# Earlier due time for the last graph, a shorter DVE hop and a shorter hold in the planner, and one activation less at the front

## The chip, the cores and the metric

The kernel runs on one core of a Trainium2 chip. A core has a matrix engine (TensorE, in the profile PE, its weight loads PEld), a vector engine (DVE), a scalar engine (ACT), a general engine (POOL) and a queue processor that only issues transfers (SP). Each engine takes its instructions in the order in which the program has them. The metric is the device time of one execution in microseconds (us), as a median of several runs.

## The reference

64 graphs of 256 nodes with 256 features each go through four layers, each behind a layer norm and a relu and each added to the residual `x`:

```
x = x + gat0(relu(ln(x)), adj)      # 4 heads, softmax over neighbours, elu
x = x + gat1(relu(ln(x)), adj)      # 4 heads, typed edges, relu, residual, layer norm per head
x = x + gat2(relu(ln(x)), adj)      # 1 head of 256
x = x + ggnn(relu(ln(x)), adj)      # 3 rounds: m = h W_i; aggr = A^T m; h = GRU(aggr, h)
```

`adj` holds only 0 and 1. No graph needs another graph, but inside a graph everything is one long chain, and the last layer is the costliest: three rounds of a GRU with six 256 x 256 products each, of which every round needs the state that the round before left.

## The kernel before

**Units.** The 64 graphs are cut into 33 units: one lone graph at the front (unit 0), 31 pairs (units 1 to 31), one lone graph at the end (unit 32). `graphs(u, first, nb)` writes down all operations of a unit: `layer0`, `layer1`, `layer2` and `gru`. A pair's operations work on 512 columns, a lone graph's on 256.

**The steps on TensorE**, with the lines by which the profile knows them. A *projection* (L1219, up to four row blocks) multiplies the turned, normed rows `ht` with the layer's weights. A *row* step (L1276) turns one column of scores into a row; it is a single short matmul. *Attend* (L1365) multiplies softmax weights `pt` with the projected rows; for the four-headed layers it uses half of the array's columns (`128*64` in the profile), two heads in one planner operation. In the GRU a *gate* product (L1587) is one planner operation of two matmuls of 512 columns, each of which the profile shows as two records; twelve gate operations make a round. *Aggregate* (L1566) is the product with the adjacency. A transpose through TensorE stands at L1180 (normed rows) and L1624 (the state of a lone graph).

**Turning a pair's rows.** For pairs in the middle, rows are not turned on TensorE: ACT copies them apart into two 16-bit planes (`pl<-xn`, `pl<-ht`, L1168), SP issues a transposing transfer (`tp<-pl`, L1197 and L1604), and ACT (for `ht`) or DVE (for `y`) joins the planes again. For the last unit (`ENDED = 1`) and for the first ones the rows go through TensorE (L1180) and one ACT copy. Between two rounds of a pair's GRU the state goes `ht`, `pl`, `tp`, `y`, `hl`, aggregate; between two rounds of the lone graph it goes L1624, `hl`, aggregate.

**The order is planned.** The kernel holds its own planner, `_Schedule`. Every operation has a cost, and a due time worked back from the end of its unit, `sched.end[u]`, through the operations that need it. The planner then plays the program through on a model of the engines: whenever an engine is idle, it takes, among the operations whose inputs are ready and whose buffers are free, the one with the earliest due time. The order in which it does this is the order in which the program issues on every engine, SP's and ACT's transfers too. The unit ends are 100000 ns apart for a pair (`PACE`), later than the kernel needs, so that they only rank the units. Two of the planner's numbers matter here. `HOP` is the time that it lets pass from the end of an operation until another engine may use the result. `HOLD` is about the array's two shapes: a change between full-width matmuls and the half-width attend costs time, so on TensorE the planner keeps to the present shape as long as there is work of that shape due no more than `HOLD` ns after the most urgent one (unless two attends of the half-width shape are waiting, `TOGETHER`).

**The front.** The DMA issues on ACT for the weight vectors, a one-column `Exp` activation named `warm` (L880), then the first norm. Every DMA issue uses one of eight completion counters in turn and waits until the transfer that used the counter before has landed.

Of the kernel before, what the change touches and what calls it, by code (L numbers as in the profile page):

```python
# [9 lines left out]
F32 = mybir.dt.float32  # L10
# [3 lines left out]
AF = mybir.ActivationFunctionType  # L14
# [521 lines left out]
LEAVE = 0  # L536
PACE = 100000.0
FIRST = 0.0
SINGLES = 1, 1
LAG = 6000  # L540

# [24 lines left out]
class _Schedule:  # L566
# [9 lines left out]


    OVERLAP = {"pe": 0, "act": 97, "dve": 81, "pool": 0, "sp": 0}
    HOP = {"pe": 300, "act": 100, "dve": 100, "pool": 100, "sp": 0}
    DMA_LATENCY = 3500  # L580
    DMA_RATE = 220.0
    DMA_AHEAD = 2000
# [4 lines left out]
    GUARDED = ("wh","cb2_")  # L587
    STRICT = ("hl",)
    STICK = 0.0
    HOLD = 10000.0  # L590
    TOGETHER = 2
    SWITCH = {True: 0.0, False: 0.0}

# [118 lines left out]
    def run(self):  # L712
# [18 lines left out]
        def post(t, kind, o):  # L731
            nonlocal count
            count += 1
            heapq.heappush(events, (t, count, kind, o))
# [6 lines left out]
        while True:  # L741
            for e in engines:
# [9 lines left out]
                if e == "pe" and not halves:  # L752
                    stick = self.HOLD if sum(ops[i].halves for _, i in able[e]) < self.TOGETHER else 0.0
                while able[e]:
# [40 lines left out]
            while events and events[0][0] == clock:  # L795
                _, _, kind, o = heapq.heappop(events)
                if kind == "free":
# [5 lines left out]
                    else:  # L803
                        post(clock + self.OVERLAP[o.engine] + self.HOP[o.engine], "done", o)
                    if o.engine == "pe":
# [13 lines left out]
def _fast_path(  # L819
# [34 lines left out]
    nc = tc.nc  # L854
# [3 lines left out]
    P = 128  # L858
# [3 lines left out]
    units = [  # L862
        *((g, 1) for g in range(SINGLES[0])),
        *((g, 2) for g in range(SINGLES[0], B - SINGLES[1], 2)),
        *((g, 1) for g in range(B - SINGLES[1], B)),
    ]
# [4 lines left out]
    consts = ctx.enter_context(tc.tile_pool(name="consts", bufs=1))  # L871
# [3 lines left out]
    ones = consts.tile([P, P], F32, name="ones")  # L875
    nc.gpsimd.memset(ones, 1.0)
    ident = consts.tile([P, P], F32, name="ident")
    make_identity(nc, ident)
    warm = consts.tile([P, 1], F32, name="warm")
    nc.scalar.activation(warm, ones[:, :1], AF.Exp)  # L880
    nhalf = consts.tile([P, C * H], F32, name="nhalf")
    nc.gpsimd.memset(nhalf, -0.5)
    viol = consts.tile([P, B + 1], F32, name="viol")
# [16 lines left out]
    sched = _Schedule(  # L900
        tc,
        {
            "xt": (slots, 6), "at": (slots, 1), "am": (slots, 6), "cap": (slots, 4),
            "cap_n": (slots, 1), "xn": (slots, 3), "ht": (slots, 2), "wh": (slots, 3),
            "cb2_": (slots, 2), "cb1_": (slots, 1), "pt": (slots, 4), "o": (slots, 2),
            "ag": (slots, 2), "ht3_": (slots, 3), 
            "hl": (slots, 2), "am_r": (slots, 1), "g": (slots, 7), "y": (slots, 2), "f": (slots, 6),
            "st": (slots, 4), "mv": (slots, 6), "row": (slots, 3), "col": (slots, 4), "rs": (slots, 10),
# [791 lines left out]

    for u, (first, nb) in enumerate(units):
        sched.group = u
        sched.end[u] = (first + nb) * PACE / 2 - (FIRST if u == 0 else 0.0)
        graphs(u, first, nb)


# [23 lines left out]
@with_exitstack  # L1730
def kernel(ctx: ExitStack, tc: tile.TileContext, *args):
    nc = tc.nc
    keep = ctx.enter_context(tc.tile_pool(name="keep", bufs=1))
    flag = keep.tile([1, 1], I32, name="flag")
    _fast_path(tc, *args, flag)
    taken = nc.values_load(flag[0:1, 0:1])
    with tc.If(taken > 0):
        _general_path(tc, *args)
# [38 lines left out]
```

## Time and profile before

| what | value |
|---|---|
| median of 3 runs | 2981.08 us (2980.25 to 2981.66) |
| the profiled execution | 2981.97 us, of which the span of its instructions 2980.2 us |
| TensorE busy | 2944.9 us, 99% |
| ACT, DVE busy | 2361.1 us (79%), 2357.4 us (79%) |
| TensorE busy in 0 to 60 us, 60 to 120 us | 45.13 of 60, 54.49 of 60 |
| TensorE busy in 300 to 2540 us | 2237.84 of 2240 |
| TensorE busy in 2700 us to the end | 267.87 of 281 |
| last TensorE instruction ends | 2973.65 us |

Section 1 of the page has the busy times, section 2 the span in 40 slices, section 4 the chain of work that ended last. In the timeline every line is one instruction or a run of like ones: when it starts, how long it lasts, the engine, the line of the kernel, the operation, `written<-read`, the shape, and in brackets how long the engine was idle just before, and what ended that.

### The profile page before, as it was taken

The page shows a single profiled execution, that of the slowest core. Times are in us where ns is not written, and L with a number is a line of the kernel's source. Part 1 is how long each engine was busy: PE and PEld are TensorE (multiplying, and loading weights), DVE is VectorE, ACT ScalarE, POOL GpSimd, SP SyncE. Part 2 cuts the span into 40 slices and gives each one's busy share as a digit, 9 for nine tenths or more (in the row PEclk, how much of TensorE's full clock was granted, in tenths as well). Part 3 has the DMA queues.
Part 4 walks back from the last instruction along what each step waited for, and adds up shares of the span by engine and source line. Part 5 has one row for each costly group of instructions (what it writes and reads, how often), then busy time and mean ns, then how long its engine had stood idle before and what let it go on. Part 6 is the DMA issues. An engine that isn't in the chain of part 4 may idle for free.

```text
span 2980.2 us, 47482 instructions
## 1 busy us (share of the span) xinstructions
PE 2944.9 (99%) x16927; PEld 1754.7 (59%) x16927; DVE 2357.4 (79%) x5605; ACT 2361.1 (79%) x4404; POOL 304.0 (10%) x315
## 2 busy tenths in 40 slices
PE   8999999999999999999999999999999999999998
PEld 6765556555555555555555565555565555555555
DVE  7968877788877789777788877888777887777764
ACT  7976887888888788787888878888887987876654
POOL 2101010111110111101010101111001010000000
PEclk9999999999999999999999999999999999999999
DMA  4322533434434333433434334344343333332211
GB/s 125 85 60 67 110 86 72 107 72 100 92 76 110 78 83 89 98 85 78 94 80 100 86 75 109 69 96 93 79 106 78 82 89 93 76 74 59 51 43 28
DMA packets 560537, 248.37 MB, mean 83 GB/s; under 512 B 487130, under 2 KB 540196, under 8 KB 560292
## 3 DMA queue, kind: packets, MB, share of 16 engines
q1 hardware_dynamic: 556320, 243.88, 35.7%
q8 instruction: 137, 2.24, 0.3%
q10 hardware_dynamic: 3972, 1.36, 0.2%
q14 instruction: 108, 0.88, 0.1%
HBM read 109.84 MB, written 17.34 MB: 43 GB/s over the span
## 4 chain that ended last, share of the span: by engine, by line
PE 96%; ACT 2%; DVE 1%; DMA 0%; issue 0%; SPq 0%; ACTq 0%
PE bank L1587 65%; PE bank L1365 12%; PE bank L1219 11%; PE bank L1566 6%; ACT ht L1168 1%; ACT g L921 1%; PE bank L1045 0%; PE bank L1254 0%; PE bank L1276 0%; PE bank L1180 0%; DMA w0e<-in_L_gnn_W_dram 0%; DVE g L921 0%; DVE o L921 0%; DVE pt L921 0%; ACT xn L1124 0%
## 5 line engine op out<-in xcount | busy, mean ns | idle before, releaser
L1587 PE MATMUL bank<-ht,whh 128*128 128x512 f32 (+1 forms) x2376 | 1048.8, 581 | 1.3 <-DVE ht L921 1.0
L1587 PE MATMUL bank<-ag,wc 128*128 128x512 f32 (+1 forms) x2376 | 1037.6, 581 | 0.0
L1587 PEld LDWEIGHTS bank<-ag,wc 128*128 128x128 f32 x2376 | 445.1, 190 | 502.3 <-issue 474.5
L1587 PEld LDWEIGHTS bank<-ht,whh 128*128 128x128 f32 x2376 | 436.1, 190 | 438.0 <-issue 408.4
L921 ACT ACTIVATE g<-bank,bg 128x512 f32<-128x512 f32 (+1 forms) x594 | 395.6, 672 | 262.4 <-PE bank L1587 253.4
L921 DVE SCALAR_TENSOR_TENSOR g<-g,g 128x512 f32<-128x512 f32 (+1 forms) x396 | 263.6, 672 | 290.4 <-ACT g L921 289.4
L1365 PEld LDWEIGHTS bank<-wh,pt 128*64 128x64 f32 (+1 forms) x8704 | 344.2, 141 | 82.3 <-issue 61.6
L1365 PE MATMUL bank<-wh,pt 128*64 128x65 f32 (+1 forms) x8704 | 375.3, 232 | 1.5 <-DVE pt L921 1.5
L921 DVE SCALAR_TENSOR_TENSOR pt<-pt,f,cap 128x256 f32<-128x256 f32 x640 | 280.9, 480 | 108.5 <-ACT pt L1339 107.9
L1339 ACT ACTIVATE pt<-cb,f 128x256 f32<-128x256 f32 x640 | 334.7, 597 | 1.7 <-PE bank L1365 1.4
L1168 ACT COPY ht<-tp 128x1024 uint16<-128x1024 uint16 x232 | 301.8, 1335 | 0.0
L921 POOL TENSOR_TENSOR mv<-mv,nhalf 128x4 f32<-128x4 f32 (+1 forms) x132 | 144.4, 1094 | 1179.5 <-DVE mv L1110 916.0
L1566 PE MATMUL bank<-am_r,hl 128*128 128x256 f32 x1536 | 246.4, 309 | 0.0
L1168 ACT COPY pl<-xn 128x1024 uint16<-128x1024 uint16 x232 | 234.9, 1043 | 0.0
L1566 PEld LDWEIGHTS bank<-am_r,hl 128*128 128x128 f32 x1536 | 198.5, 188 | 48.2 <-issue 38.7
L921 POOL TENSOR_TENSOR mean<-mean,nhalf 128x8 f32<-128x8 f32 (+1 forms) x66 | 142.2, 2161 | 793.0 <-DVE mean L921 754.8
L1124 ACT ACTIVATE xn<-xt,mv 128x256 f32<-128x256 f32 x384 | 173.4, 500 | 56.0 <-DVE mv L921 48.5
L921 ACT ACTIVATE g<-g,bg 128x512 f32<-128x512 f32 (+1 forms) x198 | 136.8, 705 | 79.2 <-DVE g L921 78.8
L1168 ACT COPY pl<-ht 128x1024 uint16<-128x1024 uint16 x186 | 191.5, 1040 | 6.1 <-DVE ht L921 5.3
L1229 ACT ACTIVATE wh<-bank,mv 128x264 f32<-128x264 f32 (+1 forms) x384 | 172.0, 482 | 29.0 <-PE bank L1219 27.0
L921 DVE BATCH_NORM_STATS2 st<-xt 128x6 f32<-128x256 f32 x512 | 185.7, 413 | 6.4 <-DMA xt<-in_x_dram 6.2
L1330 DVE TENSOR_SCALAR pt<-cb,f 128x256 f32<-128x256 f32 x512 | 184.0, 408 | 8.3 <-ACT cb L1262 4.6
(104 smaller groups left out, 3163.9 us busy)
## 6 DMA issues: line engine op xcount, KB each, us to landing
cb<-rd SPq DMA_DIRECT2D x120, 512.0 KB, 4.7
xt<-in_x_dram SPq DMA_DIRECT2D x31, 512.0 KB, 5.0
at<-in_adj_dram SPq DMA_DIRECT2D x31, 512.0 KB, 4.9
out_dram<-xt SPq DMA_DIRECT2D x31, 512.0 KB, 2.9
cb<-rd SPq DMA_DIRECT2D x34, 256.0 KB, 3.2
tp<-pl SPq DMA_TRANSPOSE x418, 3.1
cap<-cap_n SPq DMA_TRANSPOSE x128, 3.0
rd<-row ACTq DMA_DIRECT2D x60, 8.0 KB, 2.3
```

Of the source, the lines that this page charges most:

```text
L921: emit = lambda: fn(*[a() if callable(a) else a for a in args], **kw)
L1124: op("act", 505, lambda: nc.scalar.activation(view(), xt.tile[:, c, :], AF.Relu, bias=mv.tile[:, 3, c : c + 1], scale=2.0 if MERGED else 1 ...
L1168: op("act", cost, lambda: nc.scalar.copy(to(), of()), reads, writes)
L1219: nc.tensor.matmul(ps.tile[:, : heads * W], lhsT=ht.tile[:, c, dc, :], rhs=we[:, dc].rearrange("p h w -> p (h w)"), start=(dc == 0), stop= ...
L1229: op("act", 470, lambda: nc.scalar.activation(wh.tile[:, :, c, :], ps.tile[:, : heads * W].rearrange("p (h w) -> p h w", h=heads), AF.Iden ...
L1330: nc.vector.tensor_scalar(pt.tile[:, b, jc, :].rearrange("p (i n) -> p i n", n=P), cb.tile[:, k, 2 * b : 2 * b + 2, :], f.tile[:, 1, h, c ...
L1339: op("act", 590, lambda: nc.scalar.activation(view().rearrange("p (i n) -> p i n", n=P), cb.tile[:, k, 2 * b : 2 * b + 2, :], AF.Relu, sca ...
L1365: nc.tensor.matmul(ps[q * Q : (q + 1) * Q], lhsT=pt.tile[:, b, jc, i0 : i0 + Q], rhs=wh.tile[:, h, 2 * b + jc, :w], start=(jc == 0), stop= ...
L1566: nc.tensor.matmul(ps.tile[:, b * N : (b + 1) * N], lhsT=rows(k, b, sc), rhs=am.tile[:, 2 * b + sc, :], start=(k == 0 and sc == 0), stop=( ...
L1587: nc.tensor.matmul(by_chunk(ps.tile[:, :S]), lhsT=w[:, dc, g * P : (g + 1) * P], rhs=block(v, dc), start=(first and dc == 0), stop=(last a ...
```

## The change

It has four parts. The planner's end of the last unit is 20000 ns earlier (`LAST`). The planner lets 60 ns instead of 100 ns pass after a DVE operation (`HOP`). It holds a shape on TensorE for work due up to 5000 ns later instead of 10000 ns (`HOLD`). The `warm` tile and its activation are gone. Costs, buffers and the work itself stay as they are.

```diff
+LAST = 20000.0
 ...
-    HOP = {"pe": 300, "act": 100, "dve": 100, "pool": 100, "sp": 0}
+    HOP = {"pe": 300, "act": 100, "dve": 60, "pool": 100, "sp": 0}
 ...
-    HOLD = 10000.0
+    HOLD = 5000.0
 ...
-    warm = consts.tile([P, 1], F32, name="warm")
-    nc.scalar.activation(warm, ones[:, :1], AF.Exp)
 ...
     for u, (first, nb) in enumerate(units):
         sched.group = u
-        sched.end[u] = (first + nb) * PACE / 2 - (FIRST if u == 0 else 0.0)
+        sched.end[u] = (first + nb) * PACE / 2 - (FIRST if u == 0 else LAST if u == len(units) - 1 else 0.0)
         graphs(u, first, nb)
```

Since the order is planned, these few numbers reorder the whole program. The built programs show how. On TensorE the first 39 planner operations are the same. In the middle of the kernel before, units alternate between two orders; in the changed one every unit has the same. At the end of the kernel before, all but one of unit 31's gate operations are issued before the lone unit 32 issues its first one; in the changed one unit 32's first round stands between the gate operations of unit 31's last round.

## The prediction

> **What bounds the kernel now.** I read the page first for the busy shares and the chain that ended last, then the busy time by stretches, then TensorE's timeline where it isn't full.
>
> ```profile
> PE 2944.9 (99%) x16927; PEld 1754.7 (59%) x16927; DVE 2357.4 (79%) x5605; ACT 2361.1 (79%) x4404; POOL 304.0 (10%) x315
> PE 96%; ACT 2%; DVE 1%; DMA 0%; issue 0%; SPq 0%; ACTq 0%
> ```
>
> TensorE is the bound almost everywhere. The change removes no matmul (both built programs have the same ones), so it can only touch TensorE's idle time, 35 us of a span of 2980.2, and what TensorE loses between instructions without being idle. The stretches say where the idle time is: 14.9 us before 60 us, 5.5 between 60 and 120, 0.2 to 300, 2.2 in the long middle, 0.2 to 2700, the rest at the end.
>
> ```profile
> 300.00:2540.00 2240.00, 2237.84 (x12763) 1305.11 (x12761) 1818.54 (x4254) 1848.58 (x3374) 231.32 (x223) 1.00 0.39 89
> 2700.00:2981.00 281.00, 267.87 (x1230) 156.61 (x1228) 178.29 (x405) 158.06 (x278) 13.96 (x18) 0.99 0.20 46
> 0.00:60.00 60.00, 45.13 (x437) 37.03 (x438) 44.40 (x151) 41.16 (x113) 11.36 (x25) 0.97 0.47 132
> 60.00:120.00 60.00, 54.49 (x484) 47.29 (x483) 54.44 (x159) 54.34 (x140) 13.05 (x14) 0.94 0.33 82
> ```
>
> (First the stretch, its length and PE's busy time; near the end PEclk, the granted clock.) The middle's 2.2 us are one repeated wait, of the layer 1 projection for ACT's join of `ht`. It falls in every second unit, every 180.5 us, 12 times. One such unit, then one without the wait, on TensorE:
>
> ```profile
> 934.15 2.74 PE L1587 MATMUL bank<-ag,wc 128*128 128x512 f32 x6
> 936.72 0.27 PE L1276 MATMUL bank<-ident,wh 128*16 128x128 f32 x1
> 937.17 3.83 PE L1219 MATMUL bank<-w1e,ht 128*128 128x264 f32 x16 [0.18 <-ACT ht L1168]
> 940.84 0.59 PE L1587 MATMUL bank<-ht,whh 128*128 128x512 f32 x1
> ...
> 1023.75 3.60 PE L1587 MATMUL bank<-ag,wc 128*128 128x512 f32 x8
> 1027.18 3.72 PE L1219 MATMUL bank<-w1e,ht 128*128 128x264 f32 x16
> 1030.74 0.59 PE L1587 MATMUL bank<-ht,whh 128*128 128x512 f32 x1
> ```
>
> **The middle.** The wait costs more than its 0.18 us. From L1276's start to the projection's are 0.45 us, where L1276 otherwise takes 0.10 (at 929.75 the next matmul starts at 929.85); and the projection after it takes 3.67 us from start to start against 3.56. That is 0.45 us each time. In the changed order every unit has the wait-free form: after the layer 2 row step come five gate operations, then the projection; of the twelve units only unit 5 keeps the old one. So 11 of 12 go: 11 x 0.45 = **-4.95 us**.
>
> Does the form stay free of the wait? It begins earlier than before: from the end of the last layer 0 attend the projection is reached after two aggregates (1.87), eight gates (8 x 1.717 = 13.7), four layer 2 projections (3.5) and a row (0.1), 19.2 us. The free unit above took 1004.28 to 1027.18, 22.9 us, and ACT's join there ended at 1024.91, 20.6 us after the attend, later than 19.2. But that chain was stretched by ACT's order, so I walk the changed order by the rows: aggregate's copy 1.7 us after the attend, two exponentials (1.15), the other copy (0.6), two joins (2.5), to 6.0; first gate and projection copies to 7.1, four norms (1.7), three copies (1.2), two plane copies (2.0, the first done at 10.9); the transposing transfer lands 3.1 later, at 14.0; ACT passes a gate, row, factors and two tanh (which wait for DVE on gates of 12.3 and 14.1) until 15.6, and the join (1.3) ends at 16.9. The slack is 2.3 us, and 1.5 us for the second join. In the waiting unit ACT's join stood behind one more gate activation, which itself waited for TensorE (935.21); in the changed order it stands ahead of it.
>
> **HOLD and shapes.** Around a visit to half-width attends the rows lose about 0.3 us: the matmul before it takes 0.52 instead of 0.43, the last attend matmul 0.15 instead of 0.03, the first matmul after 0.53 instead of 0.43. The order before has 78 visits, the changed one 75 (the three fewer are at the end). **-0.9 us.** The shorter hold could have brought more visits; the count says it doesn't.
>
> **The front.** The table load (1.28 us) lies in the shadow of the first loads now:
>
> ```profile
> 1.21 1.28 ACT L880 ACT_TABLE_LOAD   x1 [1.21 <-PEq L1766]
> 9.70 0.33 ACTq L977 DMA_DIRECT2D mean<-in_L_gnn_b_hh_dram  x1
> 10.14 0.91 ACT L1124 ACTIVATE xn<-xt,mv 128x256 f32<-128x256 f32 x2 [7.44 <-DMA o<-in_L_gnn_a_dram]
> ```
>
> In the changed program it stands behind ACT's seven DMA issues, directly before `xn`, on the path. But the counters have moved too: the last issue (`b_hh`) waited for the `adj` load (9.70) and now waits for the first half of `w0`, which let an ACT issue go at 7.83. So the load runs about 8.2 to 9.5 and `xn` starts at 9.5 rather than 10.14: -0.6. On SP, `w1`'s two issues (3.29 and 6.22) now wait for the `x` load (6.2) and for an ACT vector load that landed by 9.35, and the first pair's `x`, behind them, goes at up to 9.7 instead of 8.93: +0.8 if it decides. DVE takes that `x` only at 15.13, after other work, so I take **-0.3**, with -0.6 and +0.8 as ends. If `xn` had to wait for the old 10.03, the table load would cost its whole 1.3.
>
> Between 85 and 115 us the order of row, transposes and gates changes. The waits there now are 0.81 (L1276), 0.19 (L1587) and 0.44 (L1219); the row step of unit 3 goes behind a round's gates, the state's first gates still wait for ACT. Ends 0 and -1.4; **-0.5**.
>
> **The end (LAST).** TensorE's idle time from 2540 us to its last instruction is 5.99 us in 13 waits. The largest:
>
> ```profile
> 2907.54 1.10 PE L1587 MATMUL bank<-ht,whh 128*128 128x512 f32 x2 [0.50 <-DVE ht L921]
> 2909.16 7.99 PE L1587 MATMUL bank<-ht,whh 128*128 128x512 f32 x18 [0.53 <-DVE ht L921]
> 2945.38 0.41 PE L1624 MATMUL bank<-ident,ht 128*128 128x128 f32 x2 [0.77 <-DVE ht L921]
> 2946.68 0.41 PE L1624 MATMUL bank<-ident,ht 128*128 128x128 f32 x2 [0.89 <-DVE ht L921]
> ```
>
> The lone graph's first round boundary (0.77 + 0.89) gets six of unit 31's gate operations (10.3 us) as cover, the wait of unit 31's last round (0.50 + 0.53) gets the lone graph's layer 2 attend (1.7), and 0.55 and 0.10 before it go too: -3.4. The other boundary and the last transposes (0.77 + 0.40, 0.77 + 0.39) stay, and so does the drain of 6.5 us after the last matmul, as the lone graph still ends last. But its work is used up sooner, and what it covered is bare: (a) between unit 29's first two rounds only a transpose (0.44) stands. From the end of a round to the new state are 2.39 us (2906.77 to 2909.16), and half a gate (0.86) can start before: 1.1 idle. (b) Between unit 31's, the lone graph's transpose and its projection follow each other directly, and ACT has a tanh (0.69) and a plane copy (1.04) to do before the join of that transpose (0.58): 2.3 less overlaps (0.2) and the transpose (0.4), 1.7 idle. (c) The same in layer 1, with the tanh alone: 0.8. Together +3.6, so the end gives **+0.2**; ends -3.4 (all of a to c covered by something I missed) and +2 (each a little longer, by DVE's orders).
>
> **Sum.** -4.95 - 0.9 - 0.3 - 0.5 + 0.2 = -6.45 us. The profiled execution took 2981.97, 0.9 above the median; on the median of 2981.08 it gives **2974.6 us**, -0.22%. What a measurement can tell from no change is about 0.2%, 6.0 us, so the border is 2975.1.
>
> **Rivals.** *The granted clock at the end.* TensorE's idle time can cost a second time:
>
> ```profile
> 81.29:84.70 3.41, 1.88 (x44) 1.40 (x42) 3.40 (x9) 3.41 (x8) 0.00 (x0) 1.00 0.34 123
> 84.70:88.12 3.42, 3.42 (x47) 3.12 (x42) 3.39 (x11) 3.42 (x9) 0.00 (x0) 0.50 0.53 81
> 88.12:91.53 3.41, 1.32 (x6) 0.81 (x5) 2.81 (x7) 3.41 (x9) 0.00 (x0) 1.00 0.88 186
> 91.53:94.94 3.41, 2.96 (x7) 2.34 (x8) 3.38 (x11) 2.70 (x4) 0.33 (x1) 0.50 0.71 198
> 2945.07:2948.48 3.41, 2.21 (x14) 1.93 (x15) 2.82 (x7) 0.82 (x4) 0.00 (x0) 1.00 0.11 37
> ```
>
> Stretches of 3.41 us with 1.5 and 2.1 us idle were each followed by one at clock 0.50; one with 1.2 idle was not. A half-clock stretch full of matmuls loses 1.7 us. Wait (b) is 1.7 us in one piece; if it falls into one stretch, the time is 2974.6 + 1.7 = 2976.3, with a second one 2978. Against it: both stretches that were punished also held half-width attends. The Trainium skill ("TensorE: Matmul & The Clock Gate", part 1) names the same free-running 3413 ns stretch, but says that the clock falls after about one whole idle stretch; by that rule (b) costs nothing more and 2974.6 stands. The rows here differ, 1.5 us of idle time in a stretch being enough, and I go by them. Chance 0.33.
>
> *The waits are moved, not removed*: as many remain at other places of the middle; then -6.45 + 4.95, **2979.6**. For it: the shorter HOP makes the planner believe in results 40 ns sooner. Against it: 2.3 us of slack. Chance 0.10.
>
> *Slower: the join comes late in every unit.* If ACT's join in the new form ended 20.6 us after the attend, as in the free unit now, TensorE would wait 1.4 us in each of 25 units: +35, 3010 us. It decides from 6.45/25 = 0.26 us a unit, a join 2.6 us later than I walked it. 2985 if it is 0.4 a unit. Chance 0.07.
>
> **Chances.** The forecast 0.50. Its own range is 2972.5 to 2975.8, and 0.42 of its 0.50 lies below 2975.1; the clock's lies above, but for 0.04, where the end itself does better. Faster 0.46, same 0.47, slower 0.07. The range, 2971.0 to 2979.6, reaches down to the end's better bound (-3.4 in place of +0.2) and up to the moved waits.
>
> **What would show it.** In the middle, no idle time of L1219 after ACT `ht` from about 560 us on, 2237.84 of 2240 rising by 2 us, and no L1219 group of 3.83 us. At the front, `xn` near 9.5 us with the table load before it. At the end, L1587 waits near 2697 and L1219 waits near 2815 and 2870, the lone graph's first L1624 without any, and a clock of 1.00 or not after 2870. It is wrong if a wait stands in every unit, or if the front loses over 2 us.

## The result, and the profile after

The changed kernel takes **2973.11 us** (median; 2972.11 to 2974.38) against 2981.22 us (2980.25 to 2981.88) of the kernel before: a ratio of **0.9972**, 95% interval 0.9965 to 0.9980, 8.1 us less. The profiled execution took 2972.63 us, of which the span is 2970.7. The forecast was 2974.6; the measured time lies 1.5 us below it, inside the forecast's own range of 2972.5 to 2975.8.

In the page of the changed kernel TensorE (PE) is busy for 7.6 us less, and the chain that ended last is TensorE's to 98% instead of 96%:

```profile
PE 2937.3 (99%) x16927; PEld 1753.7 (59%) x16927; DVE 2362.0 (80%) x5605; ACT 2362.3 (80%) x4403; POOL 289.7 (10%) x315
PE 98%; ACT 1%; DVE 1%; DMA 0%; issue 0%; ACTq 0%; SPq 0%
```

The same stretches as before (stretch, length, TensorE's busy time, and near the end of the line the granted clock):

```profile
0.00:60.00 60.00, 46.21 (x449) 38.29 (x450) 47.68 (x164) 43.52 (x119) 13.48 (x28) 1.00 0.48 132
60.00:120.00 60.00, 53.69 (x491) 46.82 (x490) 51.08 (x153) 55.00 (x143) 12.76 (x13) 0.94 0.34 82
300.00:2540.00 2240.00, 2239.81 (x12841) 1309.16 (x12840) 1825.69 (x4267) 1850.64 (x3381) 217.25 (x223) 1.00 0.38 89
2700.00:2981.00 281.00, 257.87 (x1213) 153.26 (x1211) 171.65 (x394) 160.23 (x284) 14.94 (x18) 0.99 0.19 44
```

The middle is full but for 0.19 us: that is the one wait of unit 5. To see where the 9.3 us between the two profiled executions (2981.97 and 2972.63) lie, I take four places that both traces have: TensorE's first matmul, the wait of unit 3's row step (216 to 219 us), the wait of the layer 1 projection near 2554 to 2562 us, and TensorE's last matmul.

| stretch of TensorE | before, us | after, us | difference |
|---|---|---|---|
| start to the first matmul | 10.79 | 9.70 | -1.09 |
| to unit 3's row wait (218.76 / 216.32) | 207.97 | 206.62 | -1.35 |
| to the projection's wait (2561.96 / 2554.22) | 2343.20 | 2337.90 | -5.30 |
| to the last matmul (2973.65 / 2964.31) | 411.69 | 410.09 | -1.60 |

**The middle.** Every unit behind unit 5 has the wait-free form now. On TensorE of the changed kernel, one of the units that had waited:

```profile
1019.80 3.60 PE L1586 MATMUL bank<-ag,wc 128*128 128x512 f32 x8
1023.24 3.72 PE L1218 MATMUL bank<-w1e,ht 128*128 128x264 f32 x16
1026.80 1.88 PE L1586 MATMUL bank<-ht,whh 128*128 128x512 f32 x4
```

The projection starts 3.44 us after the two gates ahead of it and takes 3.56: no lost time on either side. (Lines are one less than before, L1218 for L1219, since one of the changes took two lines out and another put one in.) Its two joins on ACT:

```profile
1019.64 1.33 ACT L1167 COPY ht<-tp 128x1024 uint16<-128x1024 uint16 x1
1022.31 1.33 ACT L1167 COPY ht<-tp 128x1024 uint16<-128x1024 uint16 x1
```

On TensorE the aggregates behind the layer 0 attend start at 1003.94. The first join ends at 1020.97, 17.0 us later, and the projection starts 19.3 us later: a slack of 2.3 us. The second join ends at 1023.64, and its half of the projection starts 1.8 us into it, at 1025.0: 1.4 us.

**The end.** All three foretold waits are there, (a) in two pieces; the lone graph's transposes (L1623) have three waits (1.45, 0.71, 0.45 us) instead of six:

```profile
2702.12 1.10 PE L1586 MATMUL bank<-ht,whh 128*128 128x512 f32 x2 [0.59 <-ACT g L920]
2703.88 4.56 PE L1586 MATMUL bank<-ht,whh 128*128 128x512 f32 x10 [0.66 <-DVE ht L920]
2821.53 2.05 PE L1218 MATMUL bank<-w1e,ht 128*128 128x264 f32 x8 [0.82 <-ACT ht L920]
2876.54 2.01 PE L1218 MATMUL bank<-w2e,ht 128*128 128x258 f32 x8 [1.76 <-ACT ht L920]
```

**The clock at the end.** The stretch of 3.41 us that holds the whole wait of 1.76 us, and the one behind it:

```profile
2873.30:2876.71 3.41, 1.65 (x8) 0.86 (x7) 2.77 (x4) 2.27 (x5) 0.00 (x0) 1.00 0.00 0
2876.71:2880.13 3.42, 3.42 (x13) 2.13 (x14) 0.75 (x1) 2.32 (x6) 0.38 (x1) 1.00 0.80 152
```

(Columns as above; 3.41 less 1.65 is the wait.) The second stretch is granted the full clock, and so is all that follows up to TensorE's last matmul.

**The front.** On ACT the last transfer issue goes out at 7.33 us instead of 9.70: it waits for the first half of `w0`, landed at 7.31, and no longer for `adj`, which in the trace of before landed at 9.68. The table load stands between the issue and the norm, and the norm still starts at 9.04 us instead of 10.14:

```profile
7.75 1.28 ACT L1123 ACT_TABLE_LOAD   x1 [7.75 <-DMA w0e<-in_L_gnn_W_dram]
9.04 0.91 ACT L1123 ACTIVATE xn<-xt,mv 128x256 f32<-128x256 f32 x2
```

### The profile page after: what moved, and what is told of

It reads as the page before. It is cut to its first block, busy times and chain, and to the rows that moved or that the text cites. A ratio compares the mean times of both kernels' runs of the same rounds, so it can differ in the third digit from the quotient of the medians.

```text
span 2970.7 us, 47269 instructions
## 1 busy us (share of the span) xinstructions
PE 2937.3 (99%) x16927; PEld 1753.7 (59%) x16927; DVE 2362.0 (80%) x5605; ACT 2362.3 (80%) x4403; POOL 289.7 (10%) x315
## 4 chain that ended last, share of the span: by engine, by line
PE 98%; ACT 1%; DVE 1%; DMA 0%; issue 0%; ACTq 0%; SPq 0%
PE bank L1586 66%; PE bank L1364 12%; PE bank L1218 12%; PE bank L1565 6%; PE bank L1044 0%; PE bank L1253 0%; PE bank L1275 0%; PE bank L1179 0%; ACT pt L1338 0%; ACT ht L1167 0%; DMA w0e<-in_L_gnn_W_dram 0%; DVE g L920 0%; ACT g L920 0%; ACT xn L1123 0%; PE bank L1623 0%
## 5 line engine op out<-in xcount | busy, mean ns | idle before, releaser
L920 POOL TENSOR_TENSOR mv<-mv,nhalf 128x4 f32<-128x4 f32 (+1 forms) x132 | 152.9, 1158 | 1282.9 <-DVE mv L1109 953.9
L1565 PE MATMUL bank<-am_r,hl 128*128 128x256 f32 x1536 | 244.5, 308 | 0.0
L1565 PEld LDWEIGHTS bank<-am_r,hl 128*128 128x128 f32 x1536 | 197.0, 188 | 47.7 <-issue 43.8
L920 POOL TENSOR_TENSOR mean<-mean,nhalf 128x8 f32<-128x8 f32 (+1 forms) x66 | 118.1, 1802 | 754.2 <-DVE mean L920 750.7
L1228 ACT ACTIVATE wh<-bank,mv 128x264 f32<-128x264 f32 (+1 forms) x384 | 165.7, 478 | 16.4 <-PE bank L1218 15.8
```

What stands on the lines that cost most here:

```text
L920: emit = lambda: fn(*[a() if callable(a) else a for a in args], **kw)
L1228: op("act", 470, lambda: nc.scalar.activation(wh.tile[:, :, c, :], ps.tile[:, : heads * W].rearrange("p (h w) -> p h w", h=heads), AF.Iden ...
L1565: nc.tensor.matmul(ps.tile[:, b * N : (b + 1) * N], lhsT=rows(k, b, sc), rhs=am.tile[:, 2 * b + sc, :], start=(k == 0 and sc == 0), stop=( ...
```

## The experiments

The theory to be tested: HOP and HOLD free the middle, `LAST` shortens the end, and the front gains through the completion counters that ACT's transfer issues wait for. Against it stand that each part has a share of its own, that the activation's removal costs its table load, and that the new waits at the end belong to `LAST`.

| kernel | median, us | before beside it, us | ratio, 95% interval |
|---|---|---|---|
| front alone | 2980.22 | 2981.34 | 0.9996 (0.9987 to 1.0005) |
| HOP alone | 3011.23 | 2981.34 | 1.0099 (1.0084 to 1.0115) |
| HOLD alone | 2983.72 | 2981.34 | 1.0008 (0.9999 to 1.0017) |
| LAST alone | 2978.15 | 2981.34 | 0.9990 (0.9981 to 0.9999) |
| all but LAST | 2975.42 | 2981.60 | 0.9980 (0.9971 to 0.9989) |
| changed, old tail | 2971.98 | 2981.60 | 0.9967 (0.9954 to 0.9979) |
| changed, late bias vectors | 2972.96 | 2981.60 | 0.9971 (0.9960 to 0.9981) |
| old tail and late bias vectors | 2972.42 | 2981.60 | 0.9969 (0.9957 to 0.9981) |
| changed, HOP 80 | 3045.13 | 2981.18 | 1.0214 (1.0201 to 1.0228) |
| changed, HOP 40 | 3007.16 | 2981.18 | 1.0087 (1.0073 to 1.0100) |
| changed, again | 2973.08 | 2981.18 | 0.9973 (0.9962 to 0.9983) |
| changed, old tail, again | 2972.59 | 2981.18 | 0.9969 (0.9957 to 0.9981) |

### The front alone

```diff
-    warm = consts.tile([P, 1], F32, name="warm")
-    nc.scalar.activation(warm, ones[:, :1], AF.Exp)
```

> Only the front's activation is taken out; the planned order is that of the kernel before. Theory (the front's gain comes through the completion counters): the table load moves from 1.2 us to directly before the first norm and costs nothing there, because ACT's last transfer issue waits for an earlier landing; the norm starts at 9.0 us as in the changed kernel instead of 10.1, TensorE's first matmul 1.1 us earlier, and the whole is about 1 us faster (2980). Rival (a hidden load was exposed): the norm starts no earlier than 10.1 us plus up to 1.3 us, the whole 0 to 1.3 us slower. In both the middle keeps its twelve waits of the layer 1 projection.

Measured: in this run's trace the norm starts at 9.14 us, behind a table load at 7.84, and TensorE's first matmul at 9.79. In the three runs with the activation that were profiled beside it the norm starts at 10.27 to 10.40. The middle keeps its 2237.82 us. ACT's last issue went out at 7.42 instead of 9.70 to 9.96, and that outweighs the load. I had expected the load to cost nothing there, but it does cost:

```profile
7.55 0.16 DVE L1108 SCALAR_TENSOR_TENSOR mv<-mv 128x2 f32<-128x2 f32 x1
7.84 1.28 ACT L1122 ACT_TABLE_LOAD   x1 [7.84 <-DMA w0e<-in_L_gnn_W_dram]
9.14 0.91 ACT L1122 ACTIVATE xn<-xt,mv 128x256 f32<-128x256 f32 x2
```

DVE has the norm's input `mv` ready at 7.71 and ACT's issues end at 7.75, so the load of 1.28 us is on the norm's path; an activation that loads the table early and leaves the counters in this order might gain about as much again (an estimate, not tried). The median is 1.1 us lower, as expected, though the interval still holds "no change".

### HOP alone and HOLD alone

```diff
-    HOP = {"pe": 300, "act": 100, "dve": 100, "pool": 100, "sp": 0}
+    HOP = {"pe": 300, "act": 100, "dve": 60, "pool": 100, "sp": 0}
```

> Only HOP of DVE from 100 to 60. Theory (HOP and HOLD work only together): the built order has 107 visits to half-width attends instead of 78, because with the long hold the heads of the attends come apart; 29 visits at 0.3 us are about +9 us, and gate products now come up for a state that DVE has not finished in some rounds, each 1 to 2.5 us, so that the whole is 10 to 30 us slower (2990 to 3010). Rival (each part adds its own share): HOP alone takes the waits of the layer 1 projection out, the middle fills up by about 5 us and the whole is 2975 to 2977.

```diff
-    HOLD = 10000.0
+    HOLD = 5000.0
```

> Only HOLD from 10000 to 5000. Theory: the projection of layer 1 still comes after four gate products and not after five, so the twelve waits for ACT's join stay (some a little shorter, as the row stands between the projection's halves), 85 visits instead of 78 cost 7 x 0.3 = 2 us, and the whole is 1 to 2 us slower (2982 to 2983). Rival (HOLD alone is what removed the waits): busy time of the middle rises by 2 us, the whole is 4 to 5 us faster (2976 to 2977).

HOP alone is 30 us slower, 1.2 us beyond the range that I had expected: the middle has 2220.87 us of TensorE in 2240. Its timeline shows both parts of the loss:

```profile
1068.69 3.95 PE L1365 MATMUL bank<-wh,pt 128*64 128x65 f32 x128
...
1076.21 2.09 PE L1365 MATMUL bank<-wh,pt 128*64 128x65 f32 x64
...
1098.20 2.82 PE L1587 MATMUL bank<-ht,whh 128*128 128x512 f32 x4 [2.43 <-DVE ht L921]
```

A visit to the half-width attends with half the usual heads in it (x64) stands apart, so there are more visits, and a gate product comes up 2.43 us before DVE has its state. Waits of gates, aggregates and row steps fill the list of idle times from 548 to 2415 us. The middle has 17 us more idle time than before; two stretches of half clock in it and 29 visits more would make up the rest of the 30 us (an estimate, at 1.7 us a stretch and 0.3 to 0.4 a visit).

HOLD alone keeps the wait in the same units, only with the row between the projection's two halves:

```profile
937.41 1.94 PE L1219 MATMUL bank<-w1e,ht 128*128 128x264 f32 x8
939.19 0.27 PE L1276 MATMUL bank<-ident,wh 128*16 128x128 f32 x1
939.58 2.05 PE L1219 MATMUL bank<-w1e,ht 128*128 128x264 f32 x8
```

The idle time there is 0.11 to 0.13 us instead of 0.18 (unit 5 keeps 0.18), but the kernel is 2.4 us slower at the median, where I had expected 1 to 2 for 7 more visits to half-width attends. Neither of the two removes the waits by itself, since HOP alone too keeps four of the twelve (at 395, 942, 1309 and 2046 us) and brings longer ones: the rival of additive parts falls.

### The last graph's due time alone

```diff
+LAST = 20000.0
 ...
-        sched.end[u] = (first + nb) * PACE / 2 - (FIRST if u == 0 else 0.0)
+        sched.end[u] = (first + nb) * PACE / 2 - (FIRST if u == 0 else LAST if u == len(units) - 1 else 0.0)
```

> Only the due time of the last graph. Theory: the order up to about 2500 us is that of the kernel before and the middle keeps its twelve waits; at the end the lone graph's first round boundary (0.77 + 0.89) and the waits of the last pair's last round (0.50 + 0.53) are covered, the lone graph's own layers stand bare in places (1.7 and 0.8), and the whole is 1 to 3 us faster (2978 to 2980). Rival (the end gives nothing, as the prediction's +0.2 has it, or is punished by the clock): 2981 to 2983, in the latter case with a stretch of half clock before the last matmul.

2978.15 us, 3.2 less than before. The middle is the old one (2237.84). From the projection's wait near 2561 us to the last matmul it takes 408.66 us, 3.03 less than before, and idle times of 0.14, 0.12, 0.55, 0.82, 1.45, 0.71 and 0.46 us are all that is left. There is no half-clock stretch before the last matmul. The prediction's wait (a) isn't among them, and (b) is half as long, 0.82. So with the old HOP and HOLD the earlier due time gains more at the end than it does in the changed kernel, as the next run shows with its number.

### HOP, HOLD and the front together, without LAST

```diff
-LAST = 20000.0
 ...
-        sched.end[u] = (first + nb) * PACE / 2 - (FIRST if u == 0 else LAST if u == len(units) - 1 else 0.0)
+        sched.end[u] = (first + nb) * PACE / 2 - (FIRST if u == 0 else 0.0)
```

(This diff and the next ones are against the changed kernel.)

> The changed kernel without the earlier due time of the last graph: HOP, HOLD and the front together. Theory (HOP and HOLD free the middle only together): the middle is that of the changed kernel, 2239.8 us busy of 2240 with one wait of the layer 1 projection left, and the whole is 1.5 to 3.2 us above the changed kernel, 2974.6 (if the earlier due time is worth less here than alone, since the changed kernel has waits at its end that the run with LAST alone has not) to 2976.3 (if it is worth the same 3.2 as alone). Rival (the parts add up): 2981.3 + 29.9 (HOP alone) + 2.4 (HOLD alone) - 1.1 (front alone) = 3012.

2975.42 us, 6.2 less than before, though its three parts alone gave -1.1, +29.9 and +2.4. It is 2.3 us above the changed kernel (not measured side by side), between the bounds of 1.5 and 3.2 that I had expected; at the end it takes 412.15 us against 410.09, so the earlier due time is worth 2.06 us there, and 3.03 with the old HOP and HOLD. The middle is that of the changed kernel, 2239.82 us of 2240. That settles the middle: it takes HOP and HOLD both, `LAST` has no part in it, and the front alone had left its twelve waits as they were.

### Is HOP a knob?

```diff
-    HOP = {"pe": 300, "act": 100, "dve": 60, "pool": 100, "sp": 0}
+    HOP = {"pe": 300, "act": 100, "dve": 80, "pool": 100, "sp": 0}
```

> The changed kernel with HOP of DVE at 80 instead of 60. Theory (60 with a HOLD of 5000 is one pair of values for which the planner falls into a regular order, no knob with a direction): the built order has 101 visits to half-width attends instead of 75; HOP alone had 107, was 30 us slower than before and lost about as much in waits as in visits, so 26 visits more at about 1 us each for both: 2995 to 3005, with waits of gate products for a state that isn't finished. Rival (a shorter hop lets results come sooner step by step): 80 lies between 100 and 60 in time too, 2973 to 2984.

```diff
-    HOP = {"pe": 300, "act": 100, "dve": 60, "pool": 100, "sp": 0}
+    HOP = {"pe": 300, "act": 100, "dve": 40, "pool": 100, "sp": 0}
```

> The changed kernel with HOP of DVE at 40 instead of 60. Theory as for 80: the built order has 96 visits instead of 75, 21 more at about 1 us each with their waits: 2990 to 3000. Rival (shorter is better, or at least no worse): 2970 to 2975.

With 80 the kernel takes 3045.13 us and with 40 it takes 3007.16, both far slower than the kernel *before*, and both slower than I expected, 80 by at least 40 us and 40 by at least 7. The middle of the run with 80:

```profile
300.00:2540.00 2240.00, 2202.25 (x12406) 1279.39 (x12405) 1758.57 (x4116) 1801.73 (x3296) 231.39 (x218) 0.99 0.39 86
```

37.8 us of TensorE's time there are idle. One wait of an attend for DVE's `pt` is 11.42 us long, near 891 us, and is followed by 13.65 us at half clock. With 101 and 96 visits in place of 75, neither has the regular order. So the value 60 isn't better because it is smaller. It is one at which the planner, with a HOLD of 5000, falls into the same order for every unit; 20 ns to either side it does not.

### The old HOP and HOLD at the end

```diff
     HOLD = 5000.0
+    TAIL = 2500000.0
+    TAIL_HOP = 100
+    TAIL_HOLD = 10000.0
 ...
-                    stick = self.HOLD if sum(ops[i].halves for _, i in able[e]) < self.TOGETHER else 0.0
+                    stick = (self.HOLD if clock < self.TAIL else self.TAIL_HOLD) if sum(ops[i].halves for _, i in able[e]) < self.TOGETHER else 0.0
 ...
-                        post(clock + self.OVERLAP[o.engine] + self.HOP[o.engine], "done", o)
+                        hop = self.TAIL_HOP if o.engine == "dve" and clock >= self.TAIL else self.HOP[o.engine]
+                        post(clock + self.OVERLAP[o.engine] + hop, "done", o)
```

> The changed kernel, but from 2500 us of the planner's own time on it plans with the old HOP (100) and HOLD (10000). Theory (the new waits at the end come from HOP and HOLD, not from LAST): the wait (a) near 2700, 1.25 us, is gone and (b) near 2870 falls from 1.76 to about 0.8, as in the run with LAST alone, idle time from 2540 us to the last instruction 4.3 us instead of 6.5, two more visits to half-width attends cost 0.6: 1.6 us faster than the changed kernel, 2971.5. Rival (the waits belong to LAST in any order): 2973, the waits (a) and (b) as in the changed kernel.

> The changed kernel once more, beside the one with the old tail on the same chip. 2973, with the waits (a) 1.25, (b) 1.76 and (c) 0.82 at its end, in every theory; what can differ is the front, by the place of the clock's stretches.

> The changed kernel with the old HOP and HOLD from 2500 us of the planner's time on, once more. Theory: 1 to 1.6 us below the changed kernel of the same call, 2971.5 to 2972. Rival: no difference that lasts, the two medians within 0.5 us.

The two places in the first run's trace:

```profile
2700.26 3.60 PE L1590 MATMUL bank<-ag,wc 128*128 128x512 f32 x8
2703.69 1.50 PE L1222 MATMUL bank<-w0e,ht 128*128 128x264 f32 x6
```

```profile
2876.67 2.01 PE L1222 MATMUL bank<-w2e,ht 128*128 128x258 f32 x8 [0.81 <-ACT ht L924]
```

No wait stands near 2700, and (b) is 0.81. So wait (a) and half of (b) belong to HOP and HOLD at the end (the two weren't tried apart there), not to `LAST`. The end takes 408.63 and 408.60 us in these two profiled executions, against 410.09 in both of the changed kernel: 1.5 us less, where I had expected 1.6. With the late bias vectors of the next experiment in both, it is 408.81 against 410.29. Of the whole, the medians show 1.1 us less in one comparison (2971.98 against 2973.11, not measured side by side) and 0.5 in the other (2972.59 against 2973.08, side by side); the ranges overlap. For the second I had expected 1 to 1.6 us, and 0.5 is what the rival allowed; still, five of the six runs with the old tail are shorter than all eight of the changed kernel. Part of what is missing is that the end after the last matmul took 0.34 us longer in both (6.68 and 6.73 against 6.34 and 6.39), and that the front varies by more than a microsecond from run to run. So the end itself is shown to be shorter; that the kernel as a whole is faster than the changed one, by half a microsecond or more, is likely but not beyond its spread.

### The bias vectors' transfers behind the first norm

```diff
-    dma("act", 1 << 12, lambda: nc.scalar.dma_start(bi.tile, bih), (), [bi], lag=LAG)
-    dma("act", 1 << 12, lambda: nc.scalar.dma_start(bh.tile, bhh), (), [bh], lag=LAG)
+    dma("act", 1 << 12, lambda: nc.scalar.dma_start(bi.tile, bih), [(B_w2, (1, "w"))], [bi], lag=LAG)
+    dma("act", 1 << 12, lambda: nc.scalar.dma_start(bh.tile, bhh), [(B_w2, (1, "w"))], [bh], lag=LAG)
```

> The changed kernel with the two transfers of the GRU's bias vectors (b_ih, b_hh) issued after the first norm instead of before it; TensorE's order is the same. Theory (at the front ACT's issues, which wait for completion counters, hold the norm back): the table load starts when x has landed, at 6.3 us, the norm at 7.8 to 7.9 instead of 9.0, TensorE's first matmul 1.2 us earlier, and the whole 0.3 to 1.2 us faster, 2971.9 to 2972.8. Rival (the first projection waits for the weights' score columns anyway, which DVE writes up to 11.8 us): TensorE starts earlier but waits longer for the projection, the whole within 0.2 us of 2973.1.

> The old tail and the late bias vectors together. If both theories hold and the places don't touch each other, 1.6 + 0.3 to 1.2 us below the changed kernel: 2970.3 to 2971.2. Rival: as the changed kernel, 2973.

The mechanism is as expected: the table load starts at 6.49 us when `x` has landed, the norm at 7.79, and TensorE's first matmul at 8.44 instead of 9.70. The time is not: 2972.96 us, 0.15 below the changed kernel. Nor did the rival's reason hold, since the projection's wait behind that matmul is 0.68 us in both. Matched matmul by matmul (the order is the same in both), the lead of 1.26 us was down to 0.14 at 24 us:

```profile
20.32:23.73 3.41, 3.41 (x10) 2.48 (x9) 3.41 (x10) 1.72 (x5) 0.68 (x2) 0.50 1.07 383
```

Here a half-clock stretch falls on full work, which in the changed kernel's trace does not happen at that place; at 97 us it was 1.25 again, since the changed kernel has a half-clock stretch more there. So the front's gain is real, and it isn't lost at the front. Then it melts slowly, 1.19 at 216 us, 0.08 at 2702, in the aggregates (L1565): each of them takes 0.9 ns longer from start to start, and the 1328 between these two places make 1.2 us. That is no chance of one trace: against the second trace of the changed kernel the same aggregates lose 1.2 us, and the run with both changes loses 1.2 us in them against the old tail alone, while two traces of one kernel agree there to 0.04 us. The order of the matmuls is the same; why the aggregates take longer stays open. With the old tail too, 2972.42 us is no better than the old tail alone, and 1.2 us above the upper end of what I had expected.

## Why the prediction was right

- **The middle, -4.95.** Right in place and size. From unit 5's wait to the wait near 2554 us it is 2161.59 us against 2166.50, -4.91. The walk through ACT gave a first join 16.9 us after the attend, a projection at 19.2 and slacks of 2.3 and 1.5; measured are 17.0, 19.3, 2.3 and 1.4. So the rival "the join comes late in every unit" was rightly held small, and "moved, not removed" too: one wait of 0.19 us is left of the twelve. (The stretch in the table above also has the 0.4 us between unit 3 and unit 5, which I had not looked at.)
- **Shapes, -0.9, and the end, +0.2.** Their sum was -0.7, measured -1.60. The three waits were foretold at 1.1, 1.7 and 0.8, and are 1.25, 1.76 and 0.82; what went is what was to go, but the lone graph's waits that were to stay grew by 0.3 in total. Idle time after the projection's wait is 6.5 us against 6.0, +0.5 where I had +0.2. The term that was mis-sized is the price of what isn't idle. TensorE's busy time at the end shrank by 2.1 us, where I had 0.9. Two prices can be fitted to the runs (busy time of the end; visits of the whole order, since all that differ between these runs are at the end; waits of the end):

| kernel | busy at the end, us | visits to half-width attends | waits |
|---|---|---|---|
| before | 405.71 | 78 | 12 |
| LAST alone | 404.36 | 77 | 7 |
| all but LAST | 405.27 | 76 | 13 |
| changed | 403.58 | 75 | 7 |
| old tail | 404.33 | 77 | 7 |

The old tail and the changed kernel differ by two visits and 0.75 us: 0.38 a visit, not 0.3. From before to the old tail, one visit and five waits make 1.38, so a wait costs 0.20 us beside its idle time. I had counted that in the middle, where I measured start to start (0.45 for an idle 0.18), and left it out at the end: three visits at 0.38 and five waits at 0.20 are the 2.1 us. That is a fit and not a proof, since these runs set the two prices. The two orders that they were not set by lie near them and not on them: all but LAST should have 405.71 - 0.76 + 0.20 = 405.15 us and has 405.27, and HOLD alone, with two visits and one wait less at its end than before, should have 404.75 and has 405.03.
- **The front, -0.3, and 85 to 115 us, -0.5.** The norm came at 9.04, not 9.5, because the half of `w0` landed 0.5 us sooner, and SP's `x` went out at 8.68, before the 8.93 of the kernel before, not after. The gain of 1.09 us stands at the first matmul. What the changed order between 85 and 115 us gives can't be told from single traces: from the first matmul to unit 3's row wait three traces with the order before took 206.98 to 208.70 us, and seven with the changed one 206.44 to 208.20. They overlap because the clock gives each two or three half-clock stretches there (206.4 to 207.3 us with two, 206.9 to 208.7 with three). The two traces that I compare have three before and two after, which flatters the change. The medians' 8.1 us less the 5.3 and 1.6 leave some 1.2 for the front, against 0.8 forecast.
- **The clock's rival, 0.33.** It did not come: 1.76 us idle in one stretch cost nothing more. The sum had left the clock out, and that came true although the reasons given for it did not hold: this part is luck. I had read out of the rows of before that 1.5 us of idle time in a stretch is enough, and had set against it that both punished stretches held half-width attends. That second reading was wrong for the stretch at 88.12 us. The timeline had put two shapes of attend into one line; the matmuls in that stretch are those of layer 2, at full width:

```profile
87.84 1.61 PE L1365 MATMUL bank<-wh,pt 128*128 128x257 f32 x6
```

So the half-width attends aren't the reason, or not the only one, and why the stretch with wait (b) went unpunished stays open. The rule that I had set against my rows (the Trainium skill, "TensorE: Matmul & The Clock Gate", part 1) gave the right time here, though the runs don't bear it out, as the last section shows.
- **The chances.** 0.46 and 0.47 for faster and the same came out nearly even because the clock's 0.33, all but 0.04 of it, and the moved waits' 0.10 lay above the border of 2975.1. The measured time is 2.0 us below it, on the forecast's side. The terms' errors did not cancel: the middle's stretch (0.4), the end (0.9) and, as far as it can be told, the front (0.4) all came out lower than forecast.

## What to carry to other kernels

Where one engine is 99% busy, price a wait from the start of the instruction before it to the start of the second one behind it, not by the idle time that the profile prints: here an idle 0.18 us cost 0.45, and at the end a wait cost by the fit some 0.2 more than it showed. A planner's constants are not knobs: two changes that are worth +30 and +2.4 us alone gave some -5 together (-6.2 with the front's part, which alone gave -1.1), and 20 ns to either side of the value gave +26 and +64, so read the order that comes out and walk the chain that ends last through it, as here with 17.0 us against 16.9. And a constant that is right for the repeating middle needn't be right for the end, where in the traces it cost 1.5 us.

## What the runs showed of the hardware

**When the clock falls.** TensorE's clock is granted in stretches of 3.41 us. In the run with HOP alone there are waits of 2.43, 2.15 and 2.44 us before gate products; two of them with what follows each:

```profile
1095.74:1099.15 3.41, 0.98 (x4) 0.50 (x4) 3.41 (x7) 1.90 (x4) 0.00 (x0) 1.00 0.34 124
1099.15:1102.56 3.41, 3.41 (x6) 1.33 (x5) 3.41 (x10) 0.93 (x1) 0.00 (x0) 0.50 0.66 126
1460.96:1464.38 3.42, 1.43 (x5) 0.35 (x3) 3.27 (x7) 1.17 (x3) 0.00 (x0) 1.00 0.44 156
1464.38:1467.79 3.41, 3.25 (x8) 1.60 (x9) 3.41 (x10) 1.99 (x2) 0.00 (x0) 1.00 0.35 66
```

2.43 us idle in one stretch halved the next one's clock, and so did 2.44 near 2200 us; 1.99 did not, nor did a wait of 2.43 near 549 us that lay across the border of two stretches. The 14 traces together, each counted from its first record of the clock to TensorE's last matmul, fit this and widen it: all 26 stretches at full clock with 2.01 us or more of idle time were followed by half clock, and none with less than 1.29 was. Of the 43 between, 11 were. Among these 11 are five with half-width attends (1.50 to 1.53 us idle), but also some without any, such as one of eight aggregates and a row step, with 1.65 us idle, in the run with HOP 40:

```profile
764.03:767.45 3.42, 1.77 (x9) 1.16 (x9) 1.44 (x2) 3.11 (x10) 0.10 (x1) 1.00 0.46 92
767.45:770.86 3.41, 2.16 (x8) 1.93 (x9) 0.69 (x1) 1.05 (x5) 0.13 (x1) 0.50 0.77 273
```

What decides between 1.3 and 2.0 us stays open. The Trainium skill ("TensorE: Matmul & The Clock Gate", part 1) asks for a whole idle stretch, which these runs contradict: only 2 of the 26 were idle throughout.

**Where the stretches lie is chance.** Their places shift from execution to execution against the program's start, so the front of one and the same kernel had two half-clock stretches in one trace of the changed kernel and three in the other. One full of matmuls loses up to 1.7 us (an estimate: half of 3.41), so the front's own gains of about a microsecond can be eaten or doubled in a single trace.
